# Products of two attention steps with v taken together, and v projected behind the second step, in an attention and gated-FFN kernel

## The chip, the cores and the metric

One NeuronCore of one Trainium2 chip runs the whole kernel. The metric is device time in microseconds (us) for one execution; the kernel before takes 617.72 us, the median of 3 runs (617.2 to 617.77). Engines are named as the profile names them: PE is TensorE (PEld its weight loads), DVE is VectorE, ACT is ScalarE, POOL is GpSimd, SP is the queue that issues most DMAs.

## What is computed

The input x has 8 sequences of 512 tokens with 256 features. Cut to what matters:

```python
xn = layernorm(x)                                  # over the 256 features
q, k, v = split(xn @ in_proj_w.T)                  # 16 heads of 16
q, k = rope(q), rope(k)
scores = (q @ k.T) * 16 ** -0.5                    # masked: 0 <= t - s < 250
s = (softmax(scores) @ v) @ out_proj_w.T
h = [xn, -xn]
h = relu(s0 * (h @ sign(k0))) * 2                  # 512 -> 1024, weights +1 or -1
h = relu(s1 * (h @ sign(k1))) * 2                  # 1024 -> 1024
g = silu(s2 * (h @ sign(k2)))                      # 1024 -> 256
out = x + s * g
```

## The kernel before

**Sequences and layers.** The sequences b = 0 to 7 are worked off one after another. For each, the FFN is a first layer `h1` (8 chunks of 128 features, weights `w0`), a second `h2` (8 chunks, weights `w1`) and a last one `z` (2 chunks u = 0, 1, weights `w2`). Activations are split into an f16 high part and an fp32r low part, so each chunk has f16 matmuls followed by fp32r ones (`layer`, L481). A chunk leaves PSUM in two reads: ACT writes the high part (`h1h`, `h2h`, L508) and DVE the low part (`h1l`, `h2l`, L506). The last layer of sequence b is done inside sequence b+1, among the chunks of its first layer; its result is scaled on DVE (`scale`, L576). In the last sequence the second layer goes by two halves of the columns (in what follows A and B).

**Attention by steps.** The 16 heads form 4 groups g of 4, and the 512 columns 4 blocks j. The windowed scores of all groups are cut into 9 steps of about 512 columns (`steps`, L682). In a step (`step`, L819), PE computes the scores (`sc`, L712, 32-row tiles of the array, two PSUM tiles of pool `ps_s`), ACT takes the exponentials in two halves into a buffer `p` (L731, pool `probs` with two buffers), and POOL masks them (L747, L754). The products of the probabilities with v (`values`, L786, 32-column tiles) go into one PSUM tile `po` (pool `ps_o`, one buffer) for each group; with them the sums of the softmax are taken through columns of ones in `v_pad`. `flush` (L812) does the products of the step before, behind the scores of the present one; so the products of step 8 come behind the scores of step 0 of the next sequence. When a group is complete, `keep` (L797) takes it out of PSUM on ACT or DVE; later come reciprocals (`invert`), a shuffle and a product on POOL (`divide`), and the output projection (`project_o`).

**v.** `project_v` (L354) computes v for 128 tokens, and ACT copies it into `v_pad`, of which there is one. A sequence's v can be written only when the products of the sequence before are done.

**PSUM.** `ps_s` has 2 tiles (two banks each), `ps_o` 1 and `ps_m` 3. `ps_m` serves h1, h2, z, v, the projections of k and q (`project`, L368) and the output projection.

**The next sequence's input.** `stats` (L245) takes mean and variance on DVE (L252 to L256) and the power -0.5 on POOL; `enough` (L261) counts. `lay_down` (L275) transposes these `moments` (L278) and writes them to DRAM, `lay_over` (L283) reads them back over all partitions (`of_all`), and `norm_turned` (L292) normalises the transposed x (`xT`, L301) and splits it (`xh` on ACT L307, `xl` on DVE L305). Then k and q are projected, rotated (`rotate`, on POOL), split (`split_hi` on ACT, `split_lo` on DVE), written to DRAM and loaded again as stacks (`stack`, L438). Sequence 0 is turned on PE instead (`turn_x`, L315), with matmuls of the identity (`warm`, L220) around it.

**The order.** It is written by hand. `run` (L226) sorts pieces by a due time in units of the plan, a sequence being `SEQ` = 42.0 long; each piece has a cost on PE that moves a clock on, and what follows a piece on other engines is put out with a delay against this clock. Every engine then works strictly in the order in which its instructions were put out. `prepare` (L446), `ffn` (L641), `last_at` and `late` (L622, L628), `divisions` (L938) and the list `everything` (L966) set the due times. `attention` (L827) puts the 9 steps in front of FFN chunks so that the PE work between them is even; it takes its places from the pieces' costs, so that the steps move when other pieces do.

In a middle sequence of the kernel before, PE's order is: scores 0, products 8 of the sequence before, h1 chunk 0, v 0, h1 1, v 1, h1 2, v 2, h1 3, scores 1, products 0, z 0, v 3, h1 4, h1 5, scores 2, products 1, h1 6, h1 7, z 1, scores 3, products 2, h2 0 and so on.

Of the kernel before, what the change touches and what calls it, by code (L numbers as in the profile page):

```python
# [34 lines left out]
def tile_attention_times_gated_ffn(  # L35
# [279 lines left out]
    def turn_x(b, t, plain=False):  # L315
# [10 lines left out]
        if not plain and t < 2:  # L326

            pt = ps_s.tile([P, 2, T], F32, tag="sc", name=f"xnT_ps_{b}_{t}")
            pt = pt[:, 0, : EC * P].rearrange("p (c q) -> p c q", c=EC)
        else:  # L330
            pt = ps_m.tile([P, EC, P], F32, tag="mm", name=f"xnT_ps_{b}_{t}")
# [14 lines left out]
        if t + 1 == NT:  # L346
            first_parts(2, 3)
# [6 lines left out]
    def project_v(b, t):  # L354
        st = states[b]
        v = ps_m.tile([P, H // 2, 2, D], F32, tag="mm", name=f"v_ps_{b}_{t}")
        for c in range(EC):
            nc.tensor.matmul(  # L358
                v.rearrange("p n s d -> p (n s d)"),
                st["xT"][:, c, ts(t, P)],  # L360
                wqkv_sb[:, c, 2 * E :],
                start=(c == 0),
                stop=(c == EC - 1),
            )
        return [(0.0, lambda: nc.scalar.copy(v_pad[:, t, :, 0:3:2, :], v))]  # L365


    def project(b, what, part):  # L368
        st = states[b]
        col = E * "qk".index(what) + P * "ab".index(part)  # L370
        if b == 0 and what == "q":
            ps = ps_s.tile([P, 2, T], F32, tag="sc", name=f"{what}{part}_ps_{b}")[:, 0]
        else:
            ps = ps_m.tile([P, T], F32, tag="mm", name=f"{what}{part}_ps_{b}")
        for c in range(EC):
            nc.tensor.matmul(  # L376
                ps, wqkv_sb[:, c, ds(col, P)], st["xT"][:, c, :],
                start=(c == 0), stop=(c == EC - 1),
            )
# [7 lines left out]
        hi_after, lo_after = (4.0, 5.1) if b else (7, 8.2) if what == "k" else (6, 7.2)  # L387
# [58 lines left out]
    def prepare(b, plain=False):  # L446
# [4 lines left out]
        else:  # L451

            at = dict(load=9, stats=9, down=10.5, over=12, norm=16.8, k=21.8, q=24.8, v=SEQ + 0.6)
            if b == 1:
                at.update(load=18.65, stats=12, down=18.64, over=19.5, norm=23, k=27, q=29)
            dp, dv = 1.5, 1.0
# [9 lines left out]
        for t in range(NT):  # L466
# [5 lines left out]
            out.append((at["v"] + dv * t, 0.87, lambda t=t: project_v(b, t)))  # L472
        for what in "kq":
            out += [
                (at[what], 1.75, lambda w=what: project(b, w, "a")),
                (at[what] + dp, 1.75, lambda w=what: project(b, w, "b")),
            ]
# [144 lines left out]
    def last_at(b, u):  # L622

        if b + 1 < B:
            return SEQ * (b + 1) + 4 * L1 * (u + 1) + 2 * L3 * u
        return SEQ * b + NF0 * L1 + NT * L3 + HALF * (u // 2 + 1) - 2 * L3 + L3 * (u % 2)

    def late(b, u):  # L628
# [3 lines left out]
        return SEQ * (b + 1) + (33.5 + 6.4 * u if b + 2 < B else 19.2 + 5.0 * u)  # L632
# [8 lines left out]
    def ffn(b):  # L641
# [3 lines left out]
        for f in range(NF0):  # L645
# [3 lines left out]
            if f % 4 == 3 and b > 0:  # L649
                now += 2 * L3  # L650
# [161 lines left out]
    def flush():  # L812
        if pending:
            *before, of_step = pending.pop()
            for f in before:
                f()
            return values(*of_step)

    def step(b, i):  # L819
        sc, n = scores(b, i)  # L820
        had = len(pending)
        more = flush() or []
# [4 lines left out]
    def attention(b, among):  # L827
# [17 lines left out]
        for g in range(NG):  # L845

            at = times[used[g - 2][-1]] + 0.01 if g > 1 else first - (
                2.0 if b == 0 else 4.0 if b == 1 else 9.0
# [8 lines left out]
    def ends_at(b):  # L857
        return SEQ * b + (30.0 if b + 1 == B else SEQ)
# [79 lines left out]
    def divisions(b):  # L938
        out = []
        for pair in range(2):  # L940
            if b + 1 < B:
                first, d = (SEQ * b + 30.0, 2.0) if pair == 0 else (SEQ * (b + 1) + 4.2, 2.0)
            else:
                first, d = SEQ * b + (20.0 if pair == 0 else 30.6), 1.3
# [16 lines left out]
    def swap():  # L961
# [5 lines left out]
        (-34.6, 0, signs), (-40.5, 0, lambda: warm(9)), (-34.7, 0, lambda: warm(2)),  # L967
        (-32.5, 0, lambda: warm(1)), (-31.0, 0, lambda: enough(0)),
        (-32.7, 0, lambda: first_parts(0, 1)),
        (19.2, 0, make_w2), (22.5, 0, swap), (SEQ * (B - 1) + 45.0, 0, add_up),  # L970
# [156 lines left out]
```

## Time and profile before

| | us |
|---|---|
| median of 3 runs | 617.72 |
| the profiled execution | 617.83 |
| its span, first to last instruction | 616.1 |
| PE busy | 598.1 |
| DVE busy | 381.7 |
| ACT busy | 294.9 |
| POOL busy | 308.8 |
| share of PE in the chain that ended last | 91% |

The profile is of one execution. Its span leaves out what lies before the first and after the last instruction, here 1.7 us. PE counts as busy while matmuls are in its pipe. A group of instructions is named by the line that issues it and by out<-in. "Idle before, releaser" tells how long an engine had stood still before an instruction and which engine's work ended that wait. The chain is followed back from the last instruction, at each step to what released it.

### The profile page before, as it was taken

How to read it: one execution, taken by the hardware profiler on the slowest of the kernel's cores; microseconds unless marked ns; L12 is line 12 of the kernel's file. 1: busy time of each engine (PE TensorE's matmuls, PEld its weight loads, DVE VectorE, ACT ScalarE, POOL GpSimd, SP SyncE). 2: the span in 40 equal slices, each digit the busy share in tenths (PEclk: the TensorE clock that was granted, in tenths of full speed). 3: DMA queues.
4: the chain of work that ended last, by engine and by line, in shares of the span. 5: the costliest groups of instructions: out<-in, count | busy, mean ns of one | idle time of the engine just before them, and what ended most of it. 6: DMA issues, size and time to landing. Idle time of an engine off the chain costs nothing.

```text
span 616.1 us, 11176 instructions
## 1 busy us (share of the span) xinstructions
PE 598.1 (97%) x4490; PEld 367.5 (60%) x4490; DVE 381.7 (62%) x606; ACT 294.9 (48%) x414; POOL 308.8 (50%) x368
## 2 busy tenths in 40 slices
PE   8898999999999999999999999999999999999995
PEld 5453556556655566655565565655565556666794
DVE  7824545665765666655846658566576566655574
ACT  4555465345444355435455454544545435644421
POOL 2943551436723465236654466254672356626642
PEclk9998999999999999999999999999999999999998
DMA  8361370325342163222533153333524216212201
GB/s 275 152 239 53 120 271 20 112 113 194 95 138 89 70 230 113 87 86 109 199 103 121 51 203 106 111 119 115 195 87 141 91 70 224 85 52 70 81 8 40
DMA packets 38061, 74.51 MB, mean 121 GB/s; under 512 B 5360, under 2 KB 13040, under 8 KB 38000
## 3 DMA queue, kind: packets, MB, share of 16 engines
q1 hardware_dynamic: 35568, 71.48, 33.5%
q10 hardware_dynamic: 2432, 2.23, 1.1%
q8 instruction: 37, 0.61, 0.4%
q14 instruction: 24, 0.20, 0.1%
HBM read 44.30 MB, written 29.39 MB: 120 GB/s over the span
## 4 chain that ended last, share of the span: by engine, by line
PE 91%; DVE 4%; POOL 2%; DMA 1%; ACT 1%; issue 1%; SPq 0%; DVEq 0%; ACTq 0%; POOLq 0%
PE h_ps L497 44%; PE po L786 11%; PE z_ps L551 9%; PE sc L712 8%; PE v_ps L358 4%; PE att_ps L895 4%; PE ka_ps L376 3%; PE qb_ps L376 2%; PE qa_ps L376 2%; PE kb_ps L376 2%; PE warm L224 1%; DMA of_all<-d 1%; ACT p L731 1%; DMA d<-moments 1%; DVE den L568 1%
## 5 line engine op out<-in xcount | busy, mean ns | idle before, releaser
L731 ACT ACTIVATE p<-sc 128x1024 f32<-128x1024 f32 (+2 forms) x144 | 138.3, 1013 | 77.9 <-PE sc L712 43.8
L747 POOL TENSOR_SCALAR_AFFINE_SELECT p<-p 128x512 f32<-128x512 f32 x128 | 91.6, 722 | 136.2 <-ACT p L731 135.7
L497 PE MATMUL h_ps<-h1l,w1l_sb 128*128 128x512 f32 (+1 forms) x576 | 146.5, 396 | 0.0
L497 PE MATMUL h_ps<-h1h,w1h_sb 128*128 128x512 f16 (+1 forms) x576 | 123.1, 357 | 0.5 <-ACT v_pad L365 0.5
L497 PEld LDWEIGHTS h_ps<-h1l,w1l_sb 128*128 128x128 f32 x576 | 100.3, 188 | 29.6 <-issue 9.3
L508 ACT ACTIVATE h2h<-h_ps 128x512 f16<-128x512 f32 (+1 forms) x72 | 39.5, 548 | 115.8 <-PE h_ps L497 115.5
L497 PEld LDWEIGHTS <-w1h_sb 128*128 128x128 f16 x576 | 51.2, 98 | 59.0 <-issue 17.8
L754 POOL TENSOR_SCALAR_AFFINE_SELECT p<-p 128x512 f32<-128x512 f32 (+1 forms) x96 | 48.8, 509 | 74.6 <-ACT p L731 72.3
L786 PE MATMUL po<-p,v_pad 128*32 128x378 f32 (+4 forms) x1216 | 77.3, 373 | 3.1 <-DVE S L810 1.2
L612 DVE RECIPROCAL den<-den 128x256 f32<-128x256 f32 (+1 forms) x32 | 52.6, 1645 | 25.2 <-POOL den L607 25.2
L712 PEld LDWEIGHTS sc<-q,k 32*128 32x128 f32 x1216 | 44.1, 184 | 31.9 <-issue 20.6
L506 DVE SCALAR_TENSOR_TENSOR h2l<-h_ps,h2h 128x512 fp32r<-128x512 f32 (+1 forms) x72 | 43.9, 610 | 30.6 <-ACT h2h L508 30.5
L712 PE MATMUL sc<-q,k 32*128 32x378 f32 (+4 forms) x1216 | 57.5, 306 | 2.2 <-ACT p L731 2.2
L506 DVE SCALAR_TENSOR_TENSOR h1l<-h_ps,h1h 128x512 fp32r<-128x512 f32 x64 | 42.7, 679 | 24.7 <-ACT h1h L508 24.7
L863 DVE RECIPROCAL S<-S 128x128 f32<-128x128 f32 x64 | 57.4, 918 | 0.0
L497 PE MATMUL h_ps<-xl,w0l_sb 128*128 128x512 f32 x128 | 52.3, 489 | 0.0
L786 PEld LDWEIGHTS po<-p,v_pad 128*32 128x32 f32 x1216 | 31.7, 109 | 32.0 <-issue 17.7
L508 ACT ACTIVATE h1h<-h_ps 128x512 f16<-128x512 f32 x64 | 38.1, 598 | 21.5 <-PE h_ps L497 21.4
L301 DVE TENSOR_TENSOR xT<-xT,of_all 128x512 f32<-128x512 f32 x28 | 22.5, 805 | 32.2 <-DMA of_all<-d 31.8
L497 PE MATMUL h_ps<-xh,w0h_sb 128*128 128x512 f16 x128 | 38.4, 381 | 0.2 <-ACT v_pad L365 0.2
L551 PE MATMUL z_ps<-h2l,w2l_sb 128*128 128x512 f32 (+1 forms) x144 | 35.8, 390 | 0.0
L358 PE MATMUL v_ps<-wqkv_sb,xT 128*128 128x256 f32 x128 | 33.1, 381 | 2.0 <-DVE h1l L506 2.0
(101 smaller groups left out, 723.5 us busy)
## 6 DMA issues: line engine op xcount, KB each, us to landing
q<-dq SPq DMA_DIRECT2D x64, 256.0 KB, 3.5
dq<-qh SPq DMA_DIRECT2D x16, 512.0 KB, 3.3
dq<-m_qa SPq DMA_DIRECT2D x16, 512.0 KB, 5.3
k<-dk SPq DMA_DIRECT2D x32, 256.0 KB, 2.8
dk<-kh SPq DMA_DIRECT2D x8, 512.0 KB, 3.5
dk<-m_ka SPq DMA_DIRECT2D x8, 512.0 KB, 2.6
x<-in_x_dram SPq DMA_DIRECT2D x30, 128.0 KB, 2.8
xT<-in_x_t_dram SPq DMA_DIRECT2D x7, 512.0 KB, 5.2
```

The source lines that it names most:

```text
L358: nc.tensor.matmul(v.rearrange("p n s d -> p (n s d)"), st["xT"][:, c, ts(t, P)], wqkv_sb[:, c, 2 * E :], start=(c == 0), stop=(c == EC - 1),)
L376: nc.tensor.matmul(ps, wqkv_sb[:, c, ds(col, P)], st["xT"][:, c, :], start=(c == 0), stop=(c == EC - 1),)
L497: nc.tensor.matmul(ph, w[p][:, c, ts(f, P)], st[src + p][:, c, cols], start=(k == 0), stop=(k == n - 1),)
L506: nc.vector.scalar_tensor_tensor(lo, ph, 0.0, hi, ALU.max, ALU.subtract)
L508: high = lambda: nc.scalar.activation(hi, ph, AF.Relu)
L551: nc.tensor.matmul(pz, w2[p][:, c, ts(f, P)], st["h2" + p][:, c, cols], start=(c == 0 and p == "h"), stop=(c == NF1 - 1 and p == "l"),)
L612: nc.vector.reciprocal(part, part)
L712: nc.tensor.matmul(sc[r // 2][:, r % 2, ds(off, n)], st["k0", g][row, ts(j, P)], st[f"q{turn}", g][row, ds(j * P + first, n)], start=(turn ...
L731: nc.scalar.activation(p[:, 2 * half : 2 * half + 2, :n], sc[half][:, :, :n], AF.Exp, scale=D ** -0.5,)
L747: nc.gpsimd.affine_select(out=block, in_=block, compare_op=ALU.is_ge, fill=0.0, base=0, pattern=[[0, 4], [1, P]], channel_multiplier=-1,)
L786: nc.tensor.matmul(po[32 * r : 32 * r + 32, ds(j * P + first, n)], v_columns(j, g, r), p_[:, r, ds(off, n)], start=(j == 0), stop=(done an ...
L863: nc.vector.reciprocal(part, part)
```

## The change

Five things are changed. `flush` leaves one step waiting in steps 0 and 1: in step 0 no products are done, in step 1 those of step 8 of the sequence before, and in step 2 those of steps 0 and 1 together. The four projections of v stand behind the second step (due 6.36, 6.37, 6.38 and 7.30 instead of 0.6 to 3.6). The chunks of the last layer stand behind h1 chunks 1 and 5 instead of 3 and 7. For sequence 0, k is projected by halves of the columns, the first half ahead of the last two tiles of x, two calls of `warm` have gone, v takes PSUM of `ps_s`, and the splits are put out earlier. Due times around sequence 1's input, the last sequence and its end are altered.

PE's order in a middle sequence becomes: scores 0, h1 0, h1 1, z 0, h1 2, scores 1, products 8 of the sequence before, h1 3, v 0, v 1, v 2, h1 4, v 3, h1 5, scores 2, products 0 and 1, z 1, h1 6, h1 7, scores 3, products 2, h2 0 and so on.

```diff
--- before.py
+++ after.py
@@ -323,7 +323,10 @@
             else:
                 for p, dt in (("h", F16), ("l", F32R)):
                     st["x" + p] = one.tile([P, EC, T], dt, tag="x" + p, name=f"x{p}_{b}")
-        if not plain and t < 2:
+        if not plain and t == 2:
+            pt = ps_o.tile([P, T], F32, tag="po", name=f"xnT_ps_{b}_{t}")
+            pt = pt[:, : EC * P].rearrange("p (c q) -> p c q", c=EC)
+        elif not plain and t < 2:
             pt = ps_s.tile([P, 2, T], F32, tag="sc", name=f"xnT_ps_{b}_{t}")
             pt = pt[:, 0, : EC * P].rearrange("p (c q) -> p c q", c=EC)
@@ -344,7 +347,7 @@
             lambda: nc.vector.scalar_tensor_tensor(lo, pt, sgnx, hi, ALU.mult, ALU.subtract),
         ]
         if t + 1 == NT:
-            first_parts(2, 3)
+            first_parts(0, 1)
     def first_parts(*tiles):
         for t in tiles:
@@ -353,7 +356,11 @@
     def project_v(b, t):
         st = states[b]
-        v = ps_m.tile([P, H // 2, 2, D], F32, tag="mm", name=f"v_ps_{b}_{t}")
+        if b == 0:
+            v = ps_s.tile([P, 2, T], F32, tag="sc", name=f"v_ps_{b}_{t}")[:, 0, :E]
+            v = v.rearrange("p (n s d) -> p n s d", s=2, d=D)
+        else:
+            v = ps_m.tile([P, H // 2, 2, D], F32, tag="mm", name=f"v_ps_{b}_{t}")
         for c in range(EC):
             nc.tensor.matmul(
                 v.rearrange("p n s d -> p (n s d)"),
@@ -365,18 +372,25 @@
         return [(0.0, lambda: nc.scalar.copy(v_pad[:, t, :, 0:3:2, :], v))]
-    def project(b, what, part):
+    def project(b, what, part, half=None):
         st = states[b]
         col = E * "qk".index(what) + P * "ab".index(part)
         if b == 0 and what == "q":
             ps = ps_s.tile([P, 2, T], F32, tag="sc", name=f"{what}{part}_ps_{b}")[:, 0]
+        elif half == 1:
+            ps = st.pop(part)
         else:
             ps = ps_m.tile([P, T], F32, tag="mm", name=f"{what}{part}_ps_{b}")
-        for c in range(EC):
-            nc.tensor.matmul(
-                ps, wqkv_sb[:, c, ds(col, P)], st["xT"][:, c, :],
-                start=(c == 0), stop=(c == EC - 1),
-            )
+            st[part] = ps
+        for cols in [slice(0, T)] if half is None else [ts(half, T // 2)]:
+            for c in range(EC):
+                nc.tensor.matmul(
+                    ps[:, cols], wqkv_sb[:, c, ds(col, P)], st["xT"][:, c, cols],
+                    start=(c == 0), stop=(c == EC - 1),
+                )
+        if half == 0:
+            return
         m = turned.tile(
             [P, 2, T], F32, tag=f"m{part}", name=f"m_{what}{part}_{b}",
@@ -384,7 +398,7 @@
         )
         st[what, part] = m
-        hi_after, lo_after = (4.0, 5.1) if b else (7, 8.2) if what == "k" else (6, 7.2)
+        hi_after, lo_after = (4.0, 5.1) if b else (4.5, 5.7) if what == "k" else (5, 6.2)
         def times(i):
             nc.vector.tensor_tensor(
@@ -450,10 +464,10 @@
             dp, dv = 1.5, 1.5
         else:
-            at = dict(load=9, stats=9, down=10.5, over=12, norm=16.8, k=21.8, q=24.8, v=SEQ + 0.6)
+            at = dict(load=9, stats=9, down=10.5, over=12, norm=16.8, k=21.8, q=24.8, v=SEQ + 6.36)
             if b == 1:
-                at.update(load=18.65, stats=12, down=18.64, over=19.5, norm=23, k=27, q=29)
-            dp, dv = 1.5, 1.0
+                at.update(load=18.65, stats=15, down=18, over=18.7, norm=24.8, k=26.6, q=28.4)
+            dp, dv = 1.5, 0.01
             at = {n: SEQ * (b - 1) + f for n, f in at.items()}
         out = [(at["stats"], 0, lambda: stats(b))]
         if "over" in at:
@@ -469,12 +483,20 @@
                     (at["norm"] + t, 0, lambda t=t: norm(b, t)),
                     (at["x"] + t, 0.25, lambda t=t: turn_x(b, t, plain)),
                 ]
-            out.append((at["v"] + dv * t, 0.87, lambda t=t: project_v(b, t)))
+            when = at["v"] + (dv * t if b == 0 or plain or t + 1 < NT else 0.94)
+            out.append((when, 0.87, lambda t=t: project_v(b, t)))
         for what in "kq":
-            out += [
-                (at[what], 1.75, lambda w=what: project(b, w, "a")),
-                (at[what] + dp, 1.75, lambda w=what: project(b, w, "b")),
-            ]
+            for n, part in enumerate("ab"):
+                if b == 0 and what == "k" and not plain:
+                    out += [
+                        (-34.3 if n == 0 else -32.95, 0.87, lambda p=part: project(b, "k", p, 0)),
+                        (at["k"] + dp * n, 0.87, lambda p=part: project(b, "k", p, 1)),
+                    ]
+                else:
+                    out.append((
+                        at[what] + dp * n, 1.75, lambda w=what, p=part: project(b, w, p),
+                    ))
         return out
@@ -622,14 +644,14 @@
     def last_at(b, u):
         if b + 1 < B:
-            return SEQ * (b + 1) + 4 * L1 * (u + 1) + 2 * L3 * u
+            return SEQ * (b + 1) + (2 + 4 * u) * L1 + 2 * L3 * u
         return SEQ * b + NF0 * L1 + NT * L3 + HALF * (u // 2 + 1) - 2 * L3 + L3 * (u % 2)
     def late(b, u):
         if b + 1 == B:
             return last_at(b, 3) + L3 + 0.9 * u
-        return SEQ * (b + 1) + (33.5 + 6.4 * u if b + 2 < B else 19.2 + 5.0 * u)
+        return SEQ * (b + 1) + (33.5 + 6.4 * u if b + 2 < B else 20.5 + 5.0 * u)
     def finish_ffn(b, u, how):
         quick.add(last_at(b, u))
@@ -646,7 +668,7 @@
             quick.add(now)
             out.append((now, L1, lambda f=f: layer(b, "h1", "x", w0, f)))
             now += L1
-            if f % 4 == 3 and b > 0:
+            if f % 4 == 1 and b > 0:
                 now += 2 * L3
         if b + 1 == B:
             for half in range(2):
@@ -809,17 +831,21 @@
                 tile_ = st[name, g // 2] = st.pop(("half", name))
                 nc.vector.scalar_tensor_tensor(tile_, po, rows, tile_, ALU.mult, ALU.add)
-    def flush():
-        if pending:
-            *before, of_step = pending.pop()
+    def flush(leave=0):
+        out = []
+        while len(pending) > leave:
+            *before, of_step = pending.pop(0)
             for f in before:
                 f()
-            return values(*of_step)
+            out += values(*of_step) or []
+        return out
     def step(b, i):
         sc, n = scores(b, i)
         had = len(pending)
-        more = flush() or []
+        more = flush(leave=1 if i < 2 else 0)
         p, masks, exps = exponentials(b, i, sc, n)
         pending.append((exps, masks, (b, i, p)))
         return [(-0.7 if had else 0.0, exps)] + more
@@ -845,7 +871,7 @@
         for g in range(NG):
             at = times[used[g - 2][-1]] + 0.01 if g > 1 else first - (
-                2.0 if b == 0 else 4.0 if b == 1 else 9.0
+                3.5 if b == 0 else 4.0 if b == 1 else 9.0
             )
             if b and g == 1:
                 at = first + 0.01
@@ -855,7 +881,7 @@
         return out
     def ends_at(b):
-        return SEQ * b + (30.0 if b + 1 == B else SEQ)
+        return SEQ * b + (33.0 if b + 1 == B else SEQ)
     def invert(b, pair, n):
@@ -939,9 +965,9 @@
         out = []
         for pair in range(2):
             if b + 1 < B:
-                first, d = (SEQ * b + 30.0, 2.0) if pair == 0 else (SEQ * (b + 1) + 4.2, 2.0)
+                first, d = (SEQ * b + 30.0, 2.0) if pair == 0 else (SEQ * (b + 1) + 6.5, 2.0)
             else:
-                first, d = SEQ * b + (20.0 if pair == 0 else 30.6), 1.3
+                first, d = SEQ * b + (22.5 if pair == 0 else 33.6), 1.3
             for n in range(4):
                 out.append((first + d * n, 0, lambda p=pair, n=n: invert(b, p, n)))
             out.append((first + d * 4, 0, lambda p=pair: divide(b, p)))
@@ -964,10 +990,10 @@
         outs = ctx.enter_context(tc.tile_pool(name="outs", bufs=1))
     everything = [
-        (-34.6, 0, signs), (-40.5, 0, lambda: warm(9)), (-34.7, 0, lambda: warm(2)),
-        (-32.5, 0, lambda: warm(1)), (-31.0, 0, lambda: enough(0)),
-        (-32.7, 0, lambda: first_parts(0, 1)),
-        (19.2, 0, make_w2), (22.5, 0, swap), (SEQ * (B - 1) + 45.0, 0, add_up),
+        (-34.6, 0, signs), (-40.5, 0, lambda: warm(9)), (-34.7, 0, lambda: warm(0)),
+        (-31.0, 0, lambda: enough(0)),
+        (-32.7, 0, lambda: first_parts(2, 3)),
+        (19.2, 0, make_w2), (22.5, 0, swap), (SEQ * (B - 1) + 47.6, 0, add_up),
     ]
     for c in range(EC):
         everything += [
```

## The prediction

> **What bounds the kernel now.** I read the busy time by sequence first (the eight sequences start at the first `sc` of each: 38.4, 89.2, 162.5 and so on, 73.25 us apart), then the chain of waits inside one middle sequence, then the timeline of the first 60 us and of the last sequence. Columns of the first view: stretch, its length, then busy time of PE, PEld, DVE, ACT, POOL, the granted clock, DMA share and GB/s.
>
> ```profile
> 0.00:99.00 99.00, 89.29 (x621) 53.25 (x622) 52.88 (x102) 55.46 (x77) 52.20 (x65) 0.98 0.50 173
> 172.20:245.45 73.25, 73.25 (x538) 43.45 (x538) 47.79 (x72) 35.00 (x49) 36.56 (x43) 1.00 0.35 123
> 540.30:616.10 75.80, 67.48 (x623) 52.65 (x622) 44.48 (x72) 27.68 (x49) 35.01 (x42) 0.98 0.16 50
> ```
>
> A middle sequence has no idle PE: there the change can only take off what PE itself spends, and any new wait is paid in full. The first 99 us have 9.7 us of idle PE. The chain of one middle sequence (start, us, what):
>
> ```profile
> 178.58 0.77 PE sc L712 x12
> 179.35 0.98 PE po L786 x16
> ...
> 186.58 0.36 PE po L786 x8
> ...
> 194.89 1.63 PE po L786 x24
> ```
>
> And the timeline around the worst gap (start, us, engine, line, what, idle before and its releaser):
>
> ```profile
> 46.30 1.42 DVE L301 TENSOR_TENSOR xT<-xT,of_all 128x512 f32<-128x512 f32 x2 [6.45 <-DMA of_all<-d]
> 47.76 0.72 ACT L307 ACTIVATE xh<-xT,sgnx 128x512 f16<-128x512 f32 x1 [4.54 <-DVE xT L301]
> 48.86 1.89 ACT L731 ACTIVATE p<-sc 128x1000 f32<-128x1000 f32 x2
> 49.91 0.33 PE L712 MATMUL sc<-q,k 32*128 32x128 f32 x2 [1.63 <-ACT p L731]
> 53.86 3.30 PE L376 MATMUL ka_ps<-xT,wqkv_sb 128*128 128x512 f32 x4
> ```
>
> ACT reached `xh` of sequence 1 before its DMA had landed and held everything queued behind it: the exponentials of step 1, hence the scores of step 2 (their PSUM is free only when these are read), hence the `po` products and `ka`. The granted clock then fell to 0.50 in 54 to 56 us, and `ka` took 3.23 us where 1.72 is usual. From the scores of step 0 (38.43) to the end of the third `po` group (58.16) went 19.7 us for 14.3 us of work.
>
> **The change, part by part.** The base is the profiled execution, 617.83 us (span 616.1), 0.11 above the median 617.72.
>
> *Products of two steps together.* `po` groups of 128, 256, 372, 500, 512, 640, 768 and 884 columns take 0.36, 0.57, 0.77, 0.98, 1.01, 1.22, 1.43 and 1.63 us in the chain: 0.21 per 128 columns and 0.15 fixed. Two groups as one save 0.15. `sc` followed straight by a full-array matmul appears once, at 38.43 to 39.15: 0.72, as when `po` follows, so step 0 without products costs nothing new. Bounds 0 (the entry is paid twice anyway) to 0.25 (with the 0.1 us that a full matmul loses behind `po`); I take 0.15, read off eight rows. z and h1 in another order cost PE nothing: z 3.61, h1 0.90 and v 0.86 from start to start, whichever comes before.
>
> *Wait for v, new, each sequence 1 to 6.* In step 1 the delayed group of the step before (0.98) now reads the very `p` buffer that the exponentials of step 1 are to write; there are two. A row of now shows such a wait: at 554.86 `p` starts 0.99 behind the `po` group that reads its buffer, that is 0.2 behind its first block. So the exponentials start 0.2 behind the group, run 1.90, and in ACT's queue behind them stand `h1h` (0.60), then the copies of v (0.37). PE meanwhile has h1 (0.91) and two v (1.72), which take the three free PSUM buffers; the third v wants a fourth at 2.63 and gets one at 0.2+1.90+0.60+0.37+0.05 = 3.12 (0.05 as between a copy and the PE at 27.08). That is 0.49, less some 0.1 for matmuls already in PE's pipe: 0.4. Bounds: 0 (another buffer is free) and 0.85 (the buffer is that of h1, free only after `h1l`, 0.69 plus 0.03 where the copy has 0.37). The copies are nearest, since a v at 166.85 started while the `h1l` of the layer two before it still ran to 167.22.
>
> *Wait for the low halves of h1, new, each sequence 1 to 6.* The second z (due 8.96) now stands just ahead of the statistics (due 9.0), so on DVE the scaling of z, which needs z whole, stands ahead of them, and behind them two reciprocals, `moments`, and only then the low halves of h1_6 and h1_7. Now the same stretch runs while PE does h1:
>
> ```profile
> 180.34 0.41 DVE L252 BATCH_NORM_STATS2 bn<-x 128x6 f32<-128x256 f32 x1
> 182.80 0.54 DVE L264 SCALAR_TENSOR_TENSOR moments<-moments,ones 128x4 f32<-128x4 f32 x1
> 183.28 1.28 DVE L506 SCALAR_TENSOR_TENSOR h1l<-h_ps,h1h 128x512 fp32r<-128x512 f32 x2
> 185.34 0.15 DVE L278 STREAM_TRANSPOSE moments<-moments 128x32 f32<-128x32 f32 x1
> ```
>
> From the end of z: 0.2 + scaling 0.66 + statistics 2.58 (180.34 to 183.28 is 2.94, with `moments` at 0.54; at 12.80 it took 0.15, and I take nearly that) + 0.86 + 0.17 + 0.86 + two low halves 1.32 = 6.65, and 0.06 to PE. PE does h1 twice, `sc`, `po` 128 (2.98), eight f16 matmuls (1.55) and wants the eighth low half 1.79 later: 6.32, or 6.46 with the pipe. Wait 0.25; bounds 0 and 0.75. Late next is `moments`, so `of_all` and `xT`: 5.6 us from transpose to landing (185.49 to 191.09) puts `xT` whole at 14.85 behind z, and `ka`'s second half wants it at 15.7: covered by 0.85; each us beyond costs one.
>
> [...] The rows agree that the neighbour counts: L264 took 0.15 with GpSimd idle, 0.54 beside a mask, 1.11 beside a weight conversion. Were it so unlucky beside the power on GpSimd, the wait would be 0.65 and the sum 2.4 higher.
>
> Middle sequences together: 6 x (0.4 + 0.25 - 0.15) = **+3.0**.
>
> *First sequence.* k by halves starts when tiles 0 and 1 are copied (8.23) and the weights have landed (8.4), not at 9.73; h1 then begins at 16.17 against 16.87: 0.7 gained, the two `warm` calls gone. The clock read 1.00 through gaps of up to 1.43 us (below), so the 0.8 us that they covered costs nothing; were it to halve the clock as at 54 us, 1.5 us.
>
> ```profile
> 27.78 1.11 DVE L264 SCALAR_TENSOR_TENSOR moments<-moments,ones 128x4 f32<-128x4 f32 x1
> ...
> 29.56 1.13 PE L358 MATMUL v_ps<-wqkv_sb,xT 128*128 128x256 f32 x4 [1.43 <-DVE h1l L506]
> ```
>
> [...]
>
> Five waits of v and h1 for `h1l` or the copy (0.15, 0.41, 0.18, 1.43, 0.46 = 2.6) go, since v gets the scores' PSUM and the statistics of sequence 1 stand behind the last h1. One takes their place: `kh`, now ahead of the second `h1h`, holds ACT until the rotation ends at 19.56; then 1.04, and on DVE `m_ka` 1.2 and `h1l` 0.69, so the fifth h1 starts at 22.75 (now 22.47). The second layer starts at about 28.1 (now 31.15). q's second half reaches DRAM 1.6 earlier, so the scores of step 0 wait for q's loads until about 36.5 (now 38.43). `moments` leaves SP behind the loads of step 0, also 1.6 earlier, so `xT` is whole at 47.4 against 51.2. ACT has the exponentials of step 1 ahead of `xh`, so steps 1 and 2 run unhindered and `ka` starts at 47.8. Next late are the exponentials of step 2 (48.8 to 50.7, behind both `xh`): scores of step 3 end at 51.2, the third `po` group at 51.75, against 58.16: 6.4 gained. The wait at 78 us (0.17+0.96, masks behind GpSimd's rotation) shrinks by some 0.6. **-7.0**, with the merged group in it; bounds -3.5 (SP's chain no earlier) and -8.
>
> *Last sequence and end.* Merged group -0.15; v's wait +0.5 (here the second v is the fourth buffer); the 1.25 us that `po` waits for DVE at 566.33 goes, as `h2` stands between, but the mask of step 5 now stands behind the gate's product on GpSimd (1.3 + 1.5 + its own 1.3): some 1.45, +0.2; the sum of the counts (0.16+0.14, hidden before) enters DVE's final run of reciprocals, less 0.14 as `total` moves behind z: +0.15. **+0.7**, bounds -1 and +2.
>
> **Sum**: 617.83 - 7.0 + 3.0 + 0.7 = 614.5, and 0.1 less for the median: **614.4**, its own range 612.5 to 616.4.
>
> **Rivals.** (1) *VectorE's queue behind z becomes the bound.* Both middle waits at their upper ends: 6 x (0.85 + 0.75 - 0.15) = 8.7, so 620.1, slower. It decides from 1.2 us a sequence on, (7.0 - 0.7)/6 + 0.15. For it: PE has no idle time to absorb anything, and DVE has 47.8 busy us of 73.25. Against: the v copies are short. (2) *The gap at 50 us is not closed*, as `of_all` lands as late as now: only 3.0 of the start is gained, 618.4, no difference. Against: the SP queue is free earlier by its rows. (3) *The middle waits do not appear* (a buffer is free, DVE keeps ahead): 617.83 - 7.0 - 6 x 0.15 + 0.7 - 0.1 = 610.5. That the merged products save nothing of themselves is possible too; it is worth 1.2 at most and shifts each case alike.
>
> **Chances.** Forecast 0.42, rival 1 0.30, rival 2 0.13, rival 3 0.15. A difference of 0.2% (1.2 us) is about what a measurement tells from none. Faster: the third rival and the forecast but for its upper edge, 0.55. Same: that edge and most of rival 2, 0.13. Slower: rival 1 and the rest, 0.32. The range 610 to 621 leaves out under 2 in 10.
>
> **What would show it.** In the changed profile: eight `po` groups a sequence, one of some 1.8 us; a v idle by about 0.4 in favour of ACT, and a low-half matmul idle by 0.25 behind DVE, in sequences 1 to 6, whose spacing would be 73.7; `ka` of sequence 1 at about 48 at full clock; the first scores near 36.5. Spacing of 74.5 or more makes rival 1 right, 73.1 rival 3, and a first sequence that still stops near 50 us rival 2.

## The result, and the profile after

The changed kernel takes 621.26 us (median of 10 runs, 618.94 to 623.08), the kernel before 617.16 us (10 runs, 615.44 to 618.29): a ratio of 1.005, 95% interval 1.0032 to 1.0067, slower by 0.5%. A second set on another occasion gave 621.47 beside 618.31, 1.0052 (1.0032 to 1.0072). The forecast was 614.4 with a range of 610 to 621. The profiled execution of the changed kernel took 619.45 us (span 617.7), 1.8 us under its median; so the stretches below tell of that execution and not of those 1.8 us.

The busy time by sequence, in the changed kernel's own stretches (first sequence, one middle sequence, last sequence; columns as before: stretch, its length, busy PE, PEld, DVE, ACT, POOL, granted clock, DMA share, GB/s):

```profile
0.00:92.50 92.50, 86.34 (x611) 52.30 (x611) 55.53 (x102) 53.45 (x72) 51.76 (x65) 0.98 0.55 185
166.40:240.43 74.03, 73.81 (x538) 43.32 (x537) 46.67 (x74) 34.56 (x49) 36.34 (x43) 1.00 0.35 122
538.70:617.70 79.00, 68.86 (x662) 53.24 (x662) 44.59 (x72) 29.51 (x52) 35.84 (x44) 0.97 0.16 49
```

The first stretch is 6.5 us shorter than its counterpart, the middle one 0.8 longer, the last 3.2 longer. The starts of each sequence's first scores, read off the timelines, split the span exactly (the third column is the mean distance from one sequence's first scores to the next's, sequences 1 to 7):

| kernel | first scores of sequence 0 | of sequence 1 | mean spacing | first scores of sequence 7 to end |
|---|---|---|---|---|
| before | 38.43 | 89.24 | 73.24 | 87.39 |
| after | 37.61 | 82.76 | 74.06 | 90.56 |
| after, second profile | 35.30 | 81.88 | 74.12 | 92.47 |

So -6.5 in the first sequence, six times +0.8 in the middle (+4.9), and +3.2 to +5.1 in the last. Of the last, 1.1 and 1.4 us are only the landing of the last store (5.2 us from its issue to the end before, 6.3 and 6.6 after); up to the end of the last matmul the last sequence takes 80.3 us before and 82.4 and 84.0 after. The gap near 50 us is closed, as this timeline of the changed kernel shows (start, us, engine, line, what, idle before and its releaser):

```profile
44.56 3.64 DVE L301 TENSOR_TENSOR xT<-xT,of_all 128x512 f32<-128x512 f32 x4 [0.62 <-DMA of_all<-d]
46.47 0.72 ACT L307 ACTIVATE xh<-xT,sgnx 128x512 f16<-128x512 f32 x1 [1.28 <-DVE xT L301]
47.66 1.92 PE L808 MATMUL po<-p,v_pad 128*32 128x378 f32 x32
49.50 1.98 PE L388 MATMUL ka_ps<-xT,wqkv_sb 128*128 128x512 f32 x4
51.42 0.79 PE L734 MATMUL sc<-q,k 32*128 32x378 f32 x16
```

`po` of the two steps together is one group of 1.84 us up to `ka`, and `ka` follows it at full clock (1.00 from 49 to 52 us; 3.23 us up to the scores before, 1.92 now); the scores of step 3 follow without a wait. In the middle sequences two waits have come, both foreseen. The first, for v (ACT's queue and PE, sequence 2):

```profile
165.79 1.90 ACT L753 ACTIVATE p<-sc 128x1000 f32<-128x1000 f32 x2 [1.17 <-PE po L808]
166.48 3.15 PE L365 MATMUL v_ps<-wqkv_sb,xT 128*128 128x256 f32 x12
167.57 0.60 ACT L530 ACTIVATE h1h<-h_ps 128x512 f16<-128x512 f32 x1
168.05 0.73 ACT L372 COPY v_pad<-v_ps 128x256 f32<-128x256 f32 x2
```

Three v should take 2.58 from start to start of what follows; they take 2.98 (to 169.46). Waits of this size inside a merged row show as its length and not in brackets. The second, for the low halves of h1 (DVE's queue behind z, and PE):

```profile
178.69 0.75 DVE L598 TENSOR_SCALAR gate<-z_ps,scales 128x512 f32<-128x512 f32 x1 [5.05 <-PE z_ps L573]
181.90 0.95 DVE L889 RECIPROCAL S<-S 128x128 f32<-128x128 f32 x1
182.98 2.69 PE L519 MATMUL h_ps<-h1l,w1l_sb 128*128 128x512 f32 x8
183.90 1.22 DVE L528 SCALAR_TENSOR_TENSOR h1l<-h_ps,h1h 128x512 fp32r<-128x512 f32 x2
185.51 1.90 PE L519 MATMUL h_ps<-h1h,w1h_sb 128*128 128x512 f16 x8
```

The eight fp32r matmuls last from 182.98 to 185.51, 2.53 where 2.04 is usual. The merged group (172.99 to 174.84, 1.85 against 0.98 and 1.01 by the rows of before) gives 0.14 back: 0.40 + 0.49 - 0.14 = 0.75 of the 0.8.

In the last sequence PE stands still for 1.70 us where it stood 1.25, and now GpSimd is what it waits for. The first line is of the kernel before, the others of the changed one:

```profile
566.33 1.50 PE L786 MATMUL po<-p,v_pad 128*32 128x378 f32 x24 [1.25 <-DVE S L810]
563.34 1.28 POOL L636 TENSOR_TENSOR gate<-gate,den 128x512 f32<-128x512 f32 x1 [2.60 <-issue]
564.70 1.49 POOL L902 TENSOR_SCALAR R<-S 128x512 f32<-128x512 f32 x1
566.27 1.18 POOL L769 TENSOR_SCALAR_AFFINE_SELECT p<-p 128x512 f32<-128x512 f32 x1
568.09 1.50 PE L808 MATMUL po<-p,v_pad 128*32 128x378 f32 x24 [1.70 <-POOL p L776]
```

Besides, the second v waits (0.85 in its row, 1.02 from start to start), and a last-layer matmul waits 0.20 for `h2l` at 603.52.

### The profile page after: what moved, and what is told of

Same layout as the page of the kernel before. It is cut to its first block, busy times and chain, and to the rows that moved or that the text cites. A ratio compares the mean times of both kernels' runs of the same rounds, so it can differ in the third digit from the quotient of the medians.

```text
span 617.7 us, 11200 instructions
## 1 busy us (share of the span) xinstructions
PE 599.3 (97%) x4492; PEld 365.9 (59%) x4492; DVE 379.6 (61%) x606; ACT 292.2 (47%) x414; POOL 309.0 (50%) x368
## 5 line engine op out<-in xcount | busy, mean ns | idle before, releaser
L519 PE MATMUL h_ps<-h1l,w1l_sb 128*128 128x512 f32 (+1 forms) x576 | 148.6, 398 | 0.6
L769 POOL TENSOR_SCALAR_AFFINE_SELECT p<-p 128x512 f32<-128x512 f32 x128 | 89.9, 709 | 116.3 <-ACT p L753 116.2
L808 PE MATMUL po<-p,v_pad 128*32 128x378 f32 (+4 forms) x1216 | 75.0, 371 | 1.8 <-POOL p L776 1.7
L598 DVE TENSOR_SCALAR gate<-z_ps,scales 128x512 f32<-128x512 f32 (+1 forms) x16 | 11.5, 717 | 45.9 <-PE z_ps L573 45.9
```

The source lines that it names most:

```text
L519: nc.tensor.matmul(ph, w[p][:, c, ts(f, P)], st[src + p][:, c, cols], start=(k == 0), stop=(k == n - 1),)
L769: nc.gpsimd.affine_select(out=block, in_=block, compare_op=ALU.is_ge, fill=0.0, base=0, pattern=[[0, 4], [1, P]], channel_multiplier=-1,)
L808: nc.tensor.matmul(po[32 * r : 32 * r + 32, ds(j * P + first, n)], v_columns(j, g, r), p_[:, r, ds(off, n)], start=(j == 0), stop=(done an ...
```

## The experiments

Thirteen runs, one of them the changed kernel again, in four sets; each set has its own runs of the kernel before beside it. Medians of 5 to 12 executions are given, beside those of before (17 to 26). The theories and rivals are those of the expectation that stands ahead of each result.

**start_only, middle_only, end_only: each part alone.** The first takes the changed kernel and puts the steady order and the end back; the other two take the kernel before and put the new order into sequences 1 to 6, or into the last one with its new due times.

```diff
 start_only, against the changed kernel (in part, with ... for what stands between; due times of the end and of the second divisions too):
-  v=SEQ + 6.36 ... dp, dv = 1.5, 0.01
+  v=SEQ + 0.6 ... dp, dv = 1.5, 1.0
-  (2 + 4 * u) * L1 + 2 * L3 * u
+  4 * L1 * (u + 1) + 2 * L3 * u
-  if f % 4 == 1 and b > 0:
+  if f % 4 == 3 and b > 0:
-  more = flush(leave=1 if i < 2 else 0)
+  more = flush(leave=1 if b == 0 and i < 2 else 0)
 middle_only, against the kernel before: the same four places new where 0 < b < B - 1, second divisions at 6.5
 end_only, against the kernel before: the same four places new where b == B - 1, second divisions at 6.5, and
-  19.2 + 5.0 * u ... 30.0 if b + 1 == B ... 20.0 if pair == 0 else 30.6 ... 45.0, 0, add_up
+  20.5 + 5.0 * u ... 33.0 if b + 1 == B ... 22.5 if pair == 0 else 33.6 ... 47.6, 0, add_up
```

> Only the first sequence of the change (k by halves, v in the scores' PSUM, the later due times of sequence 1, products of steps 0 and 1 of sequence 0 together); the other seven sequences and the end as before. Theory A (the three parts of the change add up, as the two profiles have them): first scores of sequence 1 near 82.8, spacing 73.24, so 6.5 us less than before, about 610.7 in the median. Rival B (the 2.5 us by which the medians differ more than the profiled executions do come from the start, which is unsteady since the TensorE clock falls to 0.5 at 23 us in some executions for longer or shorter): 612 to 614, with a wider scatter than before's 3 us.

> Only sequences 1 to 6 in the changed order (z after the second and sixth block of the first layer, v behind step 1, products of steps 0 and 1 together, second divisions at 6.5); first and last sequence as before. Theory A: spacing 74.05 instead of 73.24 in six sequences, +4.9, so 622.0. The prediction's sizes would give +3.0, so 620.2. Rival B2 (the unexplained 2.5 us of the medians lie in the middle sequences): 623.5 or more.

> Only the last sequence in the changed order and with its later due times. Theory A: 3.2 us from its first scores to the end more than before, 620.3. If 1.1 of that was only the landing of the last store, as the two tails suggest (6.3 against 5.2 us from the last issue to the end): 619.2. The prediction's size: +0.7, 617.9.

Beside 617.97 (23 runs): start 612.39, ratio 0.9908 (0.9878 to 0.9938); middle 623.06, 1.0081 (1.0051 to 1.0111); end 620.26, 1.0049 (1.0029 to 1.007). In microseconds -5.6, +5.1 and +2.3. The middle's spacing is 74.05, its first sequence and end those of before; the end alone takes 90.6 from its first scores. Theory A holds for the middle, and within the intervals for start and end. For the start rival B stands as well: 612.39 lies in its 612 to 614, and the profile has the slow clock (24.7 to 28.1 us), but the six executions spread 3.3 us where before's in this set spread 5.3. The sum is +1.8 where the whole shows +3.2 and +4.1; the intervals of the parts (each 1.3 to 1.9 us to either side) leave room for that, so it isn't told from this.

**stats_first: the second middle wait.**

```diff
-  at = dict(load=9, stats=9, down=10.5, ...
+  at = dict(load=9, stats=8.9, down=10.5, ...
```

> The changed kernel with the statistics of sequences 2 to 7 on VectorE ahead of the second z instead of behind it. Theory A (the low halves of h1_6 and h1_7 are late since the statistics stand behind the scaling of z): the wait of 0.49 us in the second layer's first block goes, spacing 73.55, 6 x 0.5 = 3 us less than the changed kernel, about 618.2. Rival C (the low halves wait for ScalarE's queue, and VectorE is only named as the last): spacing stays at 74.05, 621.

618.06 beside 617.97, so +0.1 where the change has +3.2 in the second set, 3.1 us less; spacing 73.54 to 73.55 in every sequence. In its timeline the statistics are done before z ends, the two low halves by 181.6, and the eight matmuls take 2.04 again:

```profile
180.38 1.22 DVE L528 SCALAR_TENSOR_TENSOR h1l<-h_ps,h1h 128x512 fp32r<-128x512 f32 x2
182.25 2.20 PE L519 MATMUL h_ps<-h1l,w1l_sb 128*128 128x512 f32 x8
184.29 1.90 PE L519 MATMUL h_ps<-h1h,w1h_sb 128*128 128x512 f16 x8
```

Theory A is shown: DVE's queue behind z, 0.5 us a sequence.

**flush_step1: is it the p buffer that makes v wait?** On top of stats_first:

```diff
-  more = flush(leave=1 if i < 2 else 0)
+  more = flush(leave=1 if i == 1 else 0)
```

> The kernel with the statistics ahead of the second z, and the products of the last step of the sequence before taken in step 0 again, so that only those of step 0 are delayed (to step 2, with step 1). Theory P (the third v waits since the exponentials of step 1 wait for the delayed products to leave their p buffer, and the copies of v stand behind them on ScalarE): the wait of 0.4 us goes, spacing 73.54 - 0.4 = 73.15, 2.4 us less in six sequences and 0.8 in the last, 614.8. Rival D (the third v waits for a PSUM buffer of the first layer, which has nothing to do with p): spacing stays at 73.54, 618.

617.42 beside 618.31; spacing 73.50. Theory P falls, and rival D has the number. The exponentials no longer wait for `po`, and v waits as before (0.37 us from start to start; the first line has the row of the exponentials, the second the three v):

```profile
164.72 1.90 ACT L753 ACTIVATE p<-sc 128x1000 f32<-128x1000 f32 x2 [0.15 <-PE sc L734]
165.45 3.11 PE L365 MATMUL v_ps<-wqkv_sb,xT 128*128 128x256 f32 x12
```

The `po` group delayed PE by about as much (0.98) as it delayed the exponentials (1.17 of idle ACT against 0.15 now), so that both now start from the scores of step 1 with the same distance. The buffer that the third v waits for is that of the first v and not, as rival D has it, one of the first layer: the third v starts 0.05 after ACT's copy of the first, here (167.38 and 167.43) and in the changed kernel (168.44 and 168.49), and that copy stands behind the exponentials and `h1h` on ACT.

**after_again: the changed kernel a second time.**

> The changed kernel once more, beside the kernel before on the same chip. Theory A (the parts add up: start -5.6, middle +5.1, end +2.3 by the medians): +1.8, about 619.8 beside 618.0. Theory W (the change adds two long waits, about 2.5 us at 20 to 23.6 us and 1.7 us in the last sequence, and an execution in which the TensorE clock falls to 0.5 for 3.4 us in one of them loses 1.7 us, in both 3.4): the median lies 3 to 4 us over before, and the mean clock of the slower executions is lower, about 0.992 against 0.995.

621.47 beside 618.31. This profile has the last sequence at 92.47, and the wait of 1.70 us is followed by a slow clock. Its clock (stretch, length, PE busy, clock, DMA share, GB/s) and the row of `po`:

```profile
566.00:567.00 1.00, 0.00 (x0) 1.00 0.00 0
568.00:569.00 1.00, 1.00 (x12) 0.50 0.00 0
569.00:570.00 1.00, 1.00 (x20) 0.50 0.06 16
570.00:571.00 1.00, 1.00 (x12) 0.52 0.67 102
```
```profile
567.57 2.79 PE L808 MATMUL po<-p,v_pad 128*32 128x378 f32 x24 [1.70 <-POOL p L776]
```

The group takes 2.72 to the next matmul, 1.44 in the first profile of the change. Of the five profiles that have this wait of 1.6 to 1.7 us (after, after_again, end_only, stats_first, flush_step1) four show the clock at 0.5 for some 3.4 us right behind it; the first profile of the change is the one that doesn't. None of the ten others shows it, eight that wait 1.23 to 1.25 there and two that don't wait. From the scores of step 6 to those of step 7 it costs 1.5 to 1.6 us (9.3 to 9.4 against 7.8). The length of the wait alone doesn't settle it: in six profiles PE waits 1.66 to 1.81 us in one piece between 20 and 27 us (middle_only, end_only, last_order, stats_first, after_old_due, kh_late), and in none of them a slow clock follows. What makes the difference isn't shown.

Theory W is right in its size, 3.2 us over before. That the slower executions have the lower clock holds only roughly (622.0 at 0.989, 619.3 at 0.995, but 622.1 at 0.993). It doesn't explain why the first profiled execution lies 1.8 under its median either: that execution had a mean clock of 0.994, and four others of the ten, at 621.2 to 621.5, had 0.994 or 0.995. This stays open.

**kh_late and rot_first: what holds the first sequence.** Both on top of start_only.

```diff
 kh_late:
-  else (4.5, 5.7) if what == "k" else (5, 6.2)
+  else (7, 8.2) if what == "k" else (5, 6.2)
 rot_first:
-  ("l", 0, -20, nc.gpsimd), ("l", 1, -19, nc.gpsimd), ("l", 2, 5.1, nc.gpsimd),
+  ("l", 0, 4.0, nc.gpsimd), ("l", 1, 9.3, nc.gpsimd), ("l", 2, 9.4, nc.gpsimd),
```

> Only the first sequence of the change, and in it the cast of kh behind the first three casts of h1 on ScalarE, as late as before the change. Theory K (kh, which waits for GpSimd's rotation until 19.6 us, holds ScalarE and with it the first layer, and the two waits it makes cost a clock window): second v near 20.9 instead of 21.4, fifth h1 near 21.8 instead of 23.6, no slow clock before 30 us, second layer near 28, first scores near 36.3; about 1.5 us less than the start alone, 610.9. Rival Q (q's way to DRAM sets the first scores whatever PE does): second layer near 28, but first scores and time as with the start alone, 612.4.

> Only the first sequence of the change, and in it GpSimd turns k before it converts the second layer's weights instead of after the first two of them (2.4 us). Theory K: rotation of k ends near 18.0 instead of 19.5, kh, the copies and q's rotation follow 1.5 us earlier, first scores near 35.5, 2 us less than the start alone, 610.4. Rival Z (VectorE, which is slowed to 2.2 to 3.5 us for the low half of k when GpSimd works beside it, is what counts): 0 to 0.5 less.

kh_late: 612.45 beside 618.31; second layer at 29.14 (31.78 with the start alone), but the second half of the first scores waits 1.52 for q's loads. Rival Q is right: once the second layer comes earlier, q's way to DRAM sets the first scores. rot_first: 608.85, ratio 0.9851 (0.9835 to 0.9866), better than expected:

```profile
15.96 2.52 POOL L425 TENSOR_TENSOR m_ka<-m_ka,m_kb 128x512 f32<-128x512 f32 x2 [8.80 <-DVE m_kb L404]
18.53 1.03 ACT L442 CAST kh<-m_ka 128x1024 fp32r<-128x1024 f32 x1
```

The rotation ends at 18.5 instead of 20.9 (start_only), first scores are at 35.20 (39.07), q's loads are issued at 30.7 (34.0), and no slow clock is seen before 600 us. The profile of start_only has that slow clock, so part of these differences is the clock; how much of the gain it is wasn't separated. This is the fastest kernel of the study, 1.5% under the kernel before.

**warm_waits: is it the idle time that slows the clock?** On top of start_only, where PE waits 2.24 and 1.06 us ahead of the second v and of the fifth block:

```diff
+  (10.69, 0, lambda: warm(3)), (10.95, 0, lambda: warm(2)),
```

> Only the first sequence of the change, with five warming matmul calls in its two long waits near 20 to 24 us (three ahead of the second v, two ahead of the fifth block of the first layer), which delay nothing. Theory W (the clock falls since PE idles 2.6 of 3.7 us there): no slow clock before 30 us in the profile, mean clock 0.996 and more, median 0.5 to 1 under the 612.4 of the start alone, and fewer executions over 613. Rival V (the clock falls whatever fills the waits, or the loss is hidden behind q's way to DRAM anyway): median 612.4 and the scatter as it was, 3 us.

611.17 beside 618.24, ratio 0.9884 (0.9868 to 0.9901), five executions within 0.75 us where start_only's six lie within 3.3 and kh_late's six, without warming, within 0.8. The waits are 0.97 and 0.62 long, and the profile has the clock at 1.00 there:

```profile
20.09 0.83 PE L224 MATMUL warm<-ident 128*128 128x128 f32 x6
24.09 0.59 PE L519 MATMUL h_ps<-xh,w0h_sb 128*128 128x512 f16 x2 [0.62 <-DVE h1l L528]
```
```profile
23.00:24.00 1.00, 0.47 (x5) 1.00 0.26 94
24.00:25.00 1.00, 0.91 (x5) 1.00 0.74 295
```

Theory W agrees with this, but it is not shown in full. For it: all five executions have a mean clock of 0.996 to 0.998, and of start_only's six five have 0.994 or 0.995. The one profile says little, as four of the six profiles of the same first sequence without warming have no slow clock there either. The gain is 1.2 us between the medians and 1.5 when each is taken against its own runs of before; the two intervals overlap, so its size isn't told.

**v0_early: two v in a row instead of three.** The start of rot_first, the new order in sequences 1 to 6 with the earlier statistics, the old end, and

```diff
+  when = SEQ * b + (1.73, 6.36, 6.37, 7.30)[t]
```

> First sequence of the change with the rotation of k ahead of the weights; sequences 1 to 6 in the changed order with the statistics ahead of the second z and the first of the four v taken before the first z, so that two and not three v stand together behind step 1; last sequence as before. Theory B4 (the third v in a row is the fourth tile that asks for a PSUM buffer, and the copies stand behind the exponentials of step 1 on ScalarE): the last 0.37 us of wait goes, spacing 73.54 - 0.37 = 73.15, which is 0.1 under the 73.24 of before; 608.85 - 0.6 = 608.3. Rival E (whatever asks for a fourth buffer behind step 1 waits for the exponentials, a first-layer block as well as a v): spacing stays at 73.5, 608.85 + 6 x 0.27 = 610.5.

616.99 beside 617.5; spacing 74.63, a full us worse than 73.54. Neither number came (608.3 and 610.5). Rival E has the mechanism right, but it counted one wait and there are two: at two places a fourth tile is asked for while the first reader of an earlier one stands behind exponentials on ACT, the last layer's `z` behind step 0 and a v behind step 1.

```profile
158.57 1.89 PE L575 MATMUL z_ps<-h2h,w2h_sb 128*128 128x512 f16 x8 [0.52 <-DVE h1l L530]
167.31 1.13 PE L365 MATMUL v_ps<-wqkv_sb,xT 128*128 128x256 f32 x4 [0.56 <-ACT v_pad L372]
```

**last_order and after_old_due: order or due times at the end?** last_order is end_only with the old due times of divisions, outputs, steps and the counts' sum. after_old_due is the changed kernel with the same old due times.

```diff
-  20.5 + 5.0 * u ... 33.0 if b + 1 == B ... 22.5 if pair == 0 else 33.6 ... 47.6, 0, add_up
+  19.2 + 5.0 * u ... 30.0 if b + 1 == B ... 20.0 if pair == 0 else 30.6 ... 45.0, 0, add_up
```

> The kernel before with the last sequence alone in the changed order, but with the old due times of its divisions, outputs, products and the counts' sum. Theory A (order and due times both cost: the v's wait 0.6 to 0.9, the low halves 0.2, against 0.5 for the mask behind the gate's product and 0.2 for the counts): the po wait in sequence 7 stays at 1.25 or is gone, +0.9 in all, 619.0 beside 618.1. Rival F (the due times alone make the loss, and the order none): 618.1.

> The changed kernel with the old due times of the last sequence (its order kept): step 5's scores come earlier among the blocks, and its masks stand ahead of the gate's product and of the count on GpSimd. Theory F (in the last sequence the due times make the loss and the order costs 0.2): the po wait of 1.70 us goes, and with it the place in the last sequence where the clock falls; 621.4 - 2.1 = 619.3, from first scores to the end about 88.5 us. Rival O (in the changed kernel the order itself makes the wait): 621.

last_order: 617.13 beside 617.5, ratio 0.9987 (0.9967 to 1.0008); the old wait of 1.25 is gone, v waits 0.56, and the last sequence takes 87.6 (87.4 before). after_old_due: 617.00 beside 618.24, ratio 0.9977 (0.9964 to 0.9989), 4.4 us less than the change when each is taken against its own runs of before; its last sequence takes 87.5:

```profile
562.12 0.63 POOL L769 TENSOR_SCALAR_AFFINE_SELECT p<-p 128x512 f32<-128x512 f32 x1 [0.98 <-ACT p L753]
563.89 1.28 POOL L636 TENSOR_TENSOR gate<-gate,den 128x512 f32<-128x512 f32 x1
564.99 1.50 PE L808 MATMUL po<-p,v_pad 128*32 128x378 f32 x24
```

The masks of step 5 stand ahead of the gate's product, and this `po` doesn't wait at all (the second v still waits 0.85). Up to the end of the last matmul the last sequence takes 79.9 us in last_order and 80.2 here, against 80.3 before and 82.4 to 84.0 in the changed kernel. Theory F is shown: the due times are the loss, and they decide the sign of the whole change. Four due times moved together; which of them does it was not tried. That this kernel gains 2.3 us more than theory F expected (619.3) is not explained.

**before_rot: the rotation alone.** The kernel before with the edit of rot_first.

> The kernel before with one edit, k turned on GpSimd ahead of the conversions of the second layer's weights. Theory K (the rotation's place holds ScalarE and VectorE in the old first sequence too): first scores at about 36.5 instead of 38.4 and 2 us less, 616.1, the gap near 50 us shorter by as much or there still. Rival G (the gap near 50 us is set by the DMA of sequence 1 and not by the first scores): first scores earlier and the time the same, 618.1.

616.06 beside 617.5, ratio 0.996 (0.9941 to 0.9978); first scores at 37.39. The gap near 50 us is still there (1.25 and 0.57 of idle PE, clock 0.69 in 50 to 60 us). So 1.4 us of the 2 that theory K expected, with the gap left, which it allowed; rival G's equal time lies outside the interval. On top of the new first sequence the same edit is worth more by the medians (3.5 to 3.9 us, rot_first against start_only), though the intervals leave room for the same gain.

## Why the prediction was wrong

The step that failed is the last term of the sum, the +0.7 for the last sequence and end: the wait behind GpSimd and that for v were priced too low, and a slow clock behind such a wait at nothing. In its place the profiles show +3.2 and +5.1. The first sequence (0.5 us), the middle (1.9) and the end (2.5 in the first profile) take the forecast from 614.4 to 619.3, where the profiled execution lies (619.45); the 1.8 us from there to the median stay open.

**What bounds the kernel** was right: a middle sequence hides nothing, and each wait there showed in full (spacings 73.99 to 74.23).

**The first sequence**, -7.0 predicted, is -6.5 by the profiles and -5.6 by start_only. The gap closed for the reasons given. Inside, the fifth h1 came at 23.61 and not 22.75, the second layer at 30.32 and not 28.1, the first scores at 37.61 and not 36.5. The term mis-sized is the low half of k on DVE, taken at 1.2: it took 2.19 beside GpSimd, and behind it the clock fell to 0.50.

```profile
20.77 2.19 DVE L449 TENSOR_TENSOR m_ka<-m_ka,kh 128x1024 fp32r<-128x1024 f32 x1
21.42 1.13 PE L365 MATMUL v_ps<-wqkv_sb,xT 128*128 128x256 f32 x4 [1.50 <-ACT v_pad L372]
23.61 1.01 PE L519 MATMUL h_ps<-xh,w0h_sb 128*128 128x512 f16 x2 [1.06 <-DVE h1l L528]
24.06 1.41 PE L519 MATMUL h_ps<-xl,w0l_sb 128*128 128x512 f32 x2
```

The 0.8 us of the two `warm` calls did cost nothing, as predicted: no slow clock before 23.08. It came with the two new waits, 1.50 and 1.06 in these lines. The prediction took the clock to stand, as it had through a gap of 1.43 us; that was one gap, and here 2.6 of 3.7 us were idle. The sum has no slow stretch in it (1.5 us by the prediction's reading of the one at 54 us); it measured 1.4.

**The middle sequences**, +3.0 predicted, are +4.9. The merged group, 0.15, measured 0.14. The wait for v, 0.4, measured 0.40, though one link of its working makes no difference: without the wait for the buffer `p` v waits 0.37 (flush_step1). The wait for the low halves, 0.25, measured 0.49 (stats_first: 0.5). There DVE's side was worked out right, 6.65 from the end of z, measured 6.69 (178.43 to 185.12); half of the error is the 0.14 by which PE's demand was moved back "with the pipe", from 6.32 to 6.46. Its demand came at 6.34. Of the rest 0.04 is DVE, and 0.08 is the eighth matmul itself, which takes 0.34 to the next where 0.25 is usual. Six times the 0.24 is most of the 1.9 us missing here.

**The last sequence and end**, +0.7 predicted, is +3.2 in the one profile and +5.1 in the other, and this is the step that turned the sign. The mechanism was named (the mask of step 5 behind the gate's product on GpSimd) and priced at +0.2; the wait measured 1.70, +0.45. The v waited 1.0 and not 0.5. The three waits that PE has there now (0.85 for v, 1.70, 0.20 for `h2l`) are 1.5 us more idle time than the 1.25 of before; up to the last matmul the sequence is 2.1 us longer, and the other 0.6 are more busy time of PE, which isn't broken down here. What was left out is that the clock fell behind this wait in four of five profiles (1.5 to 1.6 us), and that the new due times and not the new order put the gate's product there: the order by itself had set the old 1.25 free, as the prediction also says, so the two edits should have been summed apart. The landing of the last store adds noise: from its issue (on ACT's queue) to the end of the span 5.2 us before, 6.3 after, 5.1 to 6.9 in other profiles.

**The rivals.** Rival 1 named a time near the result (620.1), but not its place: spacing stayed at 74.05, under its 74.5. Rival 2 (the gap) and rival 3 (no middle waits) are excluded by 82.76 and 74.05.

## What to carry to other kernels

A change of order that comes with new due times is two changes: run each alone, since here the order of the last sequence cost nothing and due times alone cost 2.7 to 4.4 us. In a pool of three PSUM tiles, count who asks for the fourth while its reader's queue has exponentials ahead; here moving one asker made two waits of one. A PE wait as long as those here (1.6 to 1.8 us) is to be priced at its length and, as a chance, a slow stretch of clock behind it (3.4 us at 0.50): here it came in four of five profiles at one place and in none of six at another. And look, as with the rotation of k here, for a product that stands behind weight conversions on GpSimd before tuning what waits for it.

## What was not expected of the hardware

**The clock.** In the profile of the changed kernel the clock falls at 23.1 us, 3.2 after PE first ran dry, and stays low for 3.4 us (stretches of 1 us, length, PE busy, clock, DMA share, GB/s):

```profile
22.00:23.00 1.00, 0.55 (x3) 1.00 0.76 295
23.00:24.00 1.00, 0.39 (x2) 0.54 0.20 74
24.00:25.00 1.00, 1.00 (x4) 0.50 1.04 422
26.00:27.00 1.00, 1.00 (x4) 0.75 0.00 0
```

The two blocks of h1 in it take 3.18 instead of 1.80. The same instructions don't always meet it: the changed kernel (waits of 1.50 and 1.06 us) shows the slow stretch near 23 us, and flush_step1, whose first sequence is the same and waits 1.53 and 1.06 there, doesn't. Of the four other profiles of this first sequence one has both waits and the stretch (start_only), three have only the first wait, 1.09 to 1.72 long, and no stretch (after_again, stats_first, after_old_due). The length of one wait doesn't tell either, and what makes the clock fall isn't shown: in the last sequence it fell behind 1.6 to 1.7 us of idle PE in one piece in four of five profiles and behind 1.23 to 1.25 in none of eight, but here, in after_old_due, it stays at 1.00 behind 1.72.

```profile
22.08 1.13 PE L365 MATMUL v_ps<-wqkv_sb,xT 128*128 128x256 f32 x4 [1.72 <-ACT v_pad L372]
```

**GpSimd beside VectorE.** The low half of k, one instruction of 128x1024, took 1.21 to 1.22 us in three profiles, 1.37 to 1.53 in the three with the rotation moved, 2.17 to 2.19 in five and 3.49 to 3.52 in four; where it took 2.17 to 2.19, the rotation of q beside it on GpSimd took 3.46 to 3.49 instead of 2.50. In six profiles of the same new first sequence the first scores came at 35.3 to 36.1 in the three where the low half took 1.2, at 36.7 where it took 2.19 and the clock stayed at 1.00, and at 37.6 and 39.1 where it took 2.19 and the clock fell as well; so the two go with most of what the first 40 us differ by. In the three profiles with 1.21 to 1.22 the weight conversion beside it (`w1h_sb`, on GpSimd) took 2.27 to 2.29, in all others 1.19 to 1.21; where the low half took 3.49 to 3.52, conversion and rotation took 1.19 to 1.20 and 2.51. So now the one engine takes longer, now the other, now both, and what decides it isn't shown.
